# Two levels of Strassen for three quarters of the rope projections, and values weighed by half blocks

## The chip, the cores and the metric

The kernel runs on one core of a Trainium2 chip. A core has a matrix engine (PE, with a queue PEld that loads weights), a vector engine (DVE), a scalar engine (ACT), a general one (POOL), and SP, which here only issues DMAs; each queue runs its instructions in program order, and 16 DMA engines move the data. The metric is device microseconds of one execution, median of the runs shown.

## The reference

The input x is (8, 256, 512), all in float32. It is layer-normed to xn, and two branches follow:

```
q_c, k_c, v_c = up-projections (512 columns each) of 64-wide latents of xn
q_r = xn @ Wq_rope              # 512 x (128 heads * 64): the largest product by far
k_r = xn @ Wk_rope              # 64 columns, shared by the heads
scores = (q_c . k_c + q_r . k_r) / sqrt(68);  attn = softmax(scores)
s = (attn . v_c) @ Wo;   g = silu(ffn(xn));   out = x + s * g
```

The heads are 4 wide (plus 64 for the rope part), there are 128 of them, and a head's scores are 256 x 256.

## The kernel before

**First phase.** `first_phase` norms and transposes x, computes the latents and the gate g, and writes to DRAM what the second phase reads: `xs_d[p]` has, for each pair p of sequences (512 tokens), the seven operands in x of one level of Strassen's algorithm. It also runs the first four units of the projection (`Project`), since the second phase runs ahead by four.

**Second phase.** It walks over 64 blocks n = (sequence b, group sg of 16 heads), two sequences of a pair in turn, and each block in two halves; h = 2n + half numbers the 128 halves. One half does, in this order on PE: `score` twice (96 matmuls with 32 rows of weights and 256 columns each, into 4 banks of PSUM each time), for some blocks `Prepare` (q_c and k_c of a later block), and one unit j = h + 4 of the rope projection (`Chain`). An even half then also weighs the values of the whole previous block (`weigh`, `gather`). A float32 matmul shows as two instructions in the trace, so `score` twice are 96 instructions, a unit is 112, `weigh` of a block 64.

**A unit** is 256 columns of Wq_rope (two sets of 128) by 512 tokens by K = 512. `Chain` makes it of 7 products instead of 8: each has K = 256 (two chunks), 128 output rows in four tiles of 32 array columns (`on_columns`, L173), and 256 moving columns. Their sums gather in four PSUM banks: ACT copies a bank to a fresh one (`seed`) where a partial sum is wanted twice, ACT and DVE carry the four results to `qrs`. The 512 KB of weights come by `load_rope` (L124, two buffers) and the four sums of them by `sum_w`: for the first 32 units POOL computes them (L136 to L139) and SP stores them to `sums_d`; later pairs use the same columns again and load them (L142).

**The softmax** of a half: DVE takes the 8 maxima (L915) as soon as scores are there, ACT the exponentials (L921), DVE transposes them into `rings` (L928), of three slots. `some(k)` places k pairs of exponentials among ACT's copies for the projection; the order of every queue is written by hand (`manual_schedule`).

**Banks.** All PSUM tiles come from one pool of eight banks in rotation: the next one asked for waits until everything that read the bank eight requests earlier is done. An even half asks for 13, an odd one for 12.

**POOL** also builds `qcm` (L307), the masked q_c that `score` of the next block starts with, places values (L348), and adds accumulators (L980). SP's DMAs are in one queue: `load_rope` for unit j + 2 waits there until PE has finished unit j.

Of the kernel before, what the change touches and what calls it, by code (L numbers as in the profile page):

```python
# [9 lines left out]
F32 = mybir.dt.float32  # L10
# [22 lines left out]
EPS = 1e-5  # L33
QSCALE = float((HD + R) ** -0.5)
# [3 lines left out]
def mla_ffn_gate_kernel(  # L38
# [26 lines left out]
    ident = const.tile([P, P], F32, name="ident")  # L65
    make_identity(nc, ident)
# [18 lines left out]
    sums_d = [dram.tile([P, 4, 2, P], F32, name=f"sums_d{n}") for n in range(32)]  # L85
    gates_d = [dram.tile([P, D], F32, name=f"gate_d{n}") for n in range(NT // P)]

    actp = pool("act", 4)
    wp = pool("wrope", 2)
# [3 lines left out]
    wsp = pool("wsum", 2)  # L93
    xsp = pool("xsum", 1)
    qtp = pool("qt", 1)
# [10 lines left out]
    units = 4 * len(blocks) // 2  # L106
    ropes, wsums, xsums = {}, {}, {}
# [10 lines left out]

    def load_rope(j):

        if j < units:
            t = wp.tile([P, KT, 4 * R], F32, tag="w", name=f"w_{j}")
            sg, u = j // 4 % 8, j % 4
            nc.sync.dma_start(out=t, in_=w_rope[sg, u // 2][:, :, ds(u % 2 * 4 * R, 4 * R)])  # L124
            ropes[j] = t

    def sum_w(j):  # L130

        if j < units:
            t = wsp.tile([P, 4, 2, P], F32, tag="ws", name=f"ws_{j}")
            if j < 32:
                q = lambda a, k: ropes[j][:, 2 * k : 2 * k + 2, a::2]
                nc.gpsimd.tensor_add(t[:, 0], q(1, 0), q(1, 1))  # L136
                nc.gpsimd.tensor_sub(t[:, 1], t[:, 0], q(0, 0))
                nc.gpsimd.tensor_sub(t[:, 2], q(0, 0), q(1, 0))
                nc.gpsimd.tensor_sub(t[:, 3], q(0, 1), t[:, 1])  # L139
                nc.sync.dma_start(out=sums_d[j], in_=t)  # L140
            else:
                nc.sync.dma_start(out=t, in_=sums_d[j % 32])  # L142
            wsums[j] = t

    def sum_x(p, xnT):


        q = lambda k, e: xnT[:, 2 * k : 2 * k + 2, ds(e * S, S)]
        for i, of in ((0, q(0, 0)), (1, q(1, 0)), (2, q(1, 1))):
            nc.sync.dma_start(out=xs_d[p][:, i], in_=of)  # L150
        t = {i: xsp.tile([P, 2, S], F32, tag=f"x{i}", name=f"xt{i}_{p}") for i in range(3, 7)}
        for i, one, two in (
            (3, q(0, 1), q(0, 0)),
            (4, q(1, 1), t[3]),
            (5, q(1, 1), q(0, 1)),
            (6, q(1, 0), t[4]),
        ):
            nc.gpsimd.tensor_sub(t[i], one, two)
            nc.sync.dma_start(out=xs_d[p][:, i], in_=t[i])

    def load_xs(p):

        if p < B // 2:
            xsums[p] = {}
            for i in (0, 4, 5, 3, 1, 6, 2):
                xsums[p][i] = xsp.tile([P, 2, S], F32, tag=f"x{i}", name=f"x{i}_{p}")
                nc.sync.dma_start(out=xsums[p][i], in_=xs_d[p][:, i])
# [12 lines left out]
    class Project:  # L180


        def __init__(self, j):
# [3 lines left out]
            self.a = lambda a, k: w[:, 2 * k : 2 * k + 2, a::2]  # L187
            self.x = xsums[j // 32]
# [4 lines left out]
            self.banks = []  # L193
            self.e = [qtp.tile([P, S], F32, tag=f"e{i}", name=f"e{i}_{j}") for i in range(4)]
# [7 lines left out]
        def first(self):  # L202

            for i, (w, x) in enumerate(
                ((self.a(0, 0), 0), (self.s[:, 1], 4), (self.s[:, 2], 5), (self.s[:, 0], 3))
            ):
                self.banks.append(bank(f"q{i}_{self.j}")[:, 0:S])
                product(self.banks[i], w, self.x[x], True)

        def take(self, i):  # L210
            nc.scalar.copy(self.e[i], self.banks[i])

        def join(self):

            m1, m6, m7, m5 = self.e
            nc.gpsimd.tensor_add(m6, m6, m1)
            nc.gpsimd.tensor_add(m7, m7, m6)
            nc.gpsimd.tensor_add(self.out(1, 1), self.split(m7), self.split(m5))

        def second(self):  # L220

            for i, w, x in ((0, self.a(0, 1), 1), (2, self.a(1, 1), 6), (3, self.s[:, 3], 2)):
                product(self.banks[i], w, self.x[x], False)
            nc.scalar.copy(self.out(0, 0), self.split(self.banks[0]))

        def end(self):

            nc.vector.tensor_add(self.out(1, 0), self.split(self.e[1]), self.split(self.banks[2]))
            nc.vector.tensor_add(self.out(0, 1), self.split(self.e[1]), self.split(self.banks[3]))

        def start(self):
            self.first()
            for i in (0, 2, 3, 1):
                self.take(i)
            self.join()

    class Chain(Project):
# [3 lines left out]
        def __init__(self, j):  # L241
            super().__init__(j)
            self.banks = {}

        def product(self, i):

            at, w, x = {
                1: (0, self.a(0, 0), 0),
                5: (3, self.s[:, 0], 3),
                6: (1, self.s[:, 1], 4),  # L250
                2: (0, self.a(0, 1), 1),
                7: (2, self.s[:, 2], 5),
                3: (1, self.s[:, 3], 2),
                4: (2, self.a(1, 1), 6),
            }[i]
            if i in (1, 5):
                self.banks[at] = bank(f"q{at}_{self.j}")[:, 0:S]
            product(self.banks[at], w, self.x[x], i in (1, 5))
# [12 lines left out]
        def add(self, a, e):  # L271
            at = {(1, 1): 2, (0, 1): 1}[a, e]
            nc.vector.tensor_add(self.out(a, e), self.split(self.e[0]), self.split(self.banks[at]))  # L273

# [28 lines left out]
    def spread(n):  # L303

        b, sg = blocks[n]
        qcm = qcp.tile([P, 8, 4, 32], F32, tag="qcm", name=f"qcm_{n}")
        nc.gpsimd.tensor_mul(  # L307
            qcm,
            qks[b, sg // 2][0].rearrange("p (q i) -> p q i", i=32).unsqueeze(2).to_broadcast([P, 8, 4, 32]),
            mask_sb[:, ds(4 * (sg % 2), 4)].unsqueeze(1).unsqueeze(3).to_broadcast([P, 8, 4, 32]),  # L310
        )
        qcms[n] = qcm
# [39 lines left out]
    def first_phase(between):  # L352
        st = ExitStack()
        fw = pool("fw", 1, st)
        wdn_sb = fw.tile([P, KT, P], F32, name="wdn_sb")
# [389 lines left out]
        for tb in range(NTB):  # L745
            more = tb + 1 < NTB
            for u in range(6):
# [9 lines left out]
                if pj:  # L757
                    pj.second()
                    pj.end()
# [20 lines left out]
            else:  # L780
                low_out(tb, 2)
                low_sum(tb)
            gate_out(tb)
# [48 lines left out]
    def between(step):  # L832
# [4 lines left out]
        elif step == 1:  # L837
            load_act(0)
            load_act(1)
            for b in range(2):  # L840
                load_cv(b, qtp.tile([P, S], F32, tag=f"e{b}", name=f"cv_{b}"))
            for j in range(2):
                load_rope(j)
        elif step == 2:
# [4 lines left out]
            spread(0)  # L849
# [4 lines left out]
        elif step < 8:  # L854
            load_rope(step - 2)
            if step < 6:
                sum_w(step - 2)
        else:
            sum_w(4)
            sum_w(5)  # L860
            load_act(2)
# [20 lines left out]
    rings = [tp.tile([P, 3, 8, 4, 32], F32, name=f"ring{r}") for r in range(4)]  # L882
# [3 lines left out]
    def score(n, f):  # L886
# [3 lines left out]
        qcm, qr, kc, a = qcms[n], qrs[n], qks[b, sg // 2][1], acts[b]  # L890
        sc = [bank(f"sc_{n}_{f}_{r}").rearrange("p (h k) -> p h k", h=2) for r in range(4)]

        for part in range(3):
            for h in range(2):
                q = 2 * f + h
                for r in range(4):
                    rows = slice(32 * r, 32 * r + 32)
                    if part == 0:
                        lhs, rhs = qcm[rows, q], kc[rows, :]
# [26 lines left out]
    def transpose(n, f, r):  # L926

        nc.vector.transpose(  # L928
            rings[r][:, (2 * n + f // 2) % 3].rearrange("p k q i -> p q k i")[:, ds(2 * (f % 2), 2)],
# [4 lines left out]
    swapped = {}  # L934

    def weigh(n, halves=range(2)):
# [3 lines left out]
        if 0 in halves:  # L940
            avs[n] = bank(f"av_{n}")
        av = avs[n]
        slots = [(2 * n + half) % 3 for half in halves]
        if len(slots) == 2:
            one, two = sorted(slots)
            of, cols = slice(one, two + 1, two - one), ds(0, S)
            swapped[n] = one != slots[0]
        else:
            of, cols = slice(slots[0], slots[0] + 1), ds(halves[0] * P, P)
            swapped[n] = False  # L950
        for k in range(8):
            for r in range(4):
                nc.tensor.matmul(  # L953
                    av[32 * r : 32 * r + 32, cols],
                    vpad[:, k, r, :],
                    rings[r][:, of, k].rearrange("p h q i -> p h (q i)"),
# [5 lines left out]
    def gather(n, cols=ds(0, S)):  # L962


        b, sg = blocks[n]
        if n not in accs:
            accs[n] = [
                smp.tile([P, S], F32, tag=f"acc{what}{sg % 2}{b % 2}", name=f"acc{what}_{n}", bufs=1)
                for what in range(2)
            ]  # L970
        for what in (1, 0):
            side = (sg + what) % 2
            for to, of in ((early, late), (late, early)) if swapped[n] else ((cols, cols),):
                nc.scalar.activation(  # L974
                    accs[n][what][:, to], avs[n][:, of], AF.Copy, scale=sides_sb[:, side : side + 1]
                )
        if sg % 2:
# [4 lines left out]
    def normalize(n, cols=ds(0, S)):  # L982
# [5 lines left out]
        if n not in recs:  # L988
# [4 lines left out]
        nc.vector.scalar_tensor_tensor(  # L993
            outT[b][:, sg // 2, cols], x[:, cols], 1.0, rec, ALU.mult, ALU.mult
        )
# [46 lines left out]
    for n, (b, sg) in enumerate(blocks):  # L1042
        for half in range(2):
            one, two = 2 * half, 2 * half + 1
            j = 2 * n + half + 4
# [6 lines left out]
            score(n, two)  # L1052
            pre = None
# [11 lines left out]
            pj = Chain(j) if j < units else None  # L1065
            some(5 if pre else 3)
            if pj:
# [3 lines left out]
            some(1)  # L1071
            if pj:
# [4 lines left out]
            if pre:  # L1077
                pre.take()
            else:
                some(1)  # L1080
            if pj:
                pj.give(0, 0)
            some(1)
# [140 lines left out]
```

## Time and profile before

| what | us |
|---|---|
| median of 3 runs (1972.31 to 1972.64) | 1972.62 |
| the profiled execution, its own time | 1973.39 |
| its span, first to last instruction | 1971.5 |
| PE busy in the span | 1959.1 (99%) |
| DVE, ACT, POOL busy | 1576.8, 1120.1, 489.3 |
| first score of half 0 / half 4 / half 25 / half 27 / half 123 | 208.5 / 258.2 / 542.8 / 569.4 / 1900.3 |
| DMA: moved, share of the 16 engines on SP's queue | 186.95 MB, 27.6% |

"Busy" counts an engine's instructions, not its use: PE's instructions overlap, and so their durations (379 ns for one of 256 columns) say less than the distance between their starts. The half starts are those of the first matmul at L902 of each half.

### The profile page before, as it was taken

Reading aid. Unit: us, or ns where it says so; the run is one execution under the profiler, and the core shown is the slowest. Engines: PE = TensorE matmul, PEld = TensorE weight load, DVE = VectorE, ACT = ScalarE, POOL = GpSimd, SP = SyncE. Lnnn points to the kernel's source line nnn. Section 1 sums busy time; section 2 is a strip of 40 time slices with the busy share of each in tenths; the row PEclk is TensorE's granted clock in tenths of the full one; section 3 lists DMA queues with packets and bytes.
Section 4 is the critical chain, followed back from the end, with each engine's and each line's share of the span. In section 5 each row is a group of like instructions: output and inputs, shape, how many; then the busy total and the mean of one; then the engine's idle time right before and its main releaser. Section 6 shows DMA issues by size and latency. Waiting matters only on the chain.

```text
span 1971.5 us, 77380 instructions
## 1 busy us (share of the span) xinstructions
PE 1959.1 (99%) x34007; PEld 1296.3 (66%) x34007; DVE 1576.8 (80%) x2662; ACT 1120.1 (57%) x3031; POOL 489.3 (25%) x741
## 2 busy tenths in 40 slices
PE   9999999999999999999999999999999999999998
PEld 4335677676677666676776766776776767676675
DVE  7764678888887877888887877788787878888888
ACT  4433565655665654656656655556556555655664
POOL 7867343343321112110111111111111111110112
PEclk9999999999999999999999999999999999999999
DMA  6344322222232223222232223222232322122212
GB/s 196 114 136 164 121 98 77 77 83 82 84 118 90 78 92 119 78 88 86 68 125 76 92 87 121 81 88 69 85 118 75 100 88 88 66 88 88 74 49 87
DMA packets 120069, 186.95 MB, mean 95 GB/s; under 512 B 10777, under 2 KB 84905, under 8 KB 119733
## 3 DMA queue, kind: packets, MB, share of 16 engines
q1 hardware_dynamic: 119665, 181.97, 27.6%
q8 instruction: 269, 4.41, 1.0%
q14 instruction: 67, 0.55, 0.1%
q0 software_dynamic: 64, 0.01, 0.0%
q10 hardware_dynamic: 4, 0.01, 0.0%
HBM read 147.86 MB, written 34.10 MB: 92 GB/s over the span
## 4 chain that ended last, share of the span: by engine, by line
PE 95%; DVE 2%; POOL 1%; DMA 1%; issue 1%; ACT 0%; SPq 0%; ACTq 0%; POOLq 0%; DVEq 0%
PE q L173 40%; PE sc L902 34%; PE av L953 11%; PE po L173 2%; PE pf L173 2%; PE py L173 1%; PE px L173 1%; PE pm L173 1%; DVE ring L928 1%; PE qq L287 1%; PE pp L173 1%; DVE nmx L915 1%; PE first L694 0%; PE vps L332 0%; PE pm L647 0%
## 5 line engine op out<-in xcount | busy, mean ns | idle before, releaser
L921 ACT ACTIVATE pr<-sc,nmx 128x256 f32<-128x256 f32 x2048 | 805.4, 495 | 386.2 <-DVE nmx L915 384.5
L915 DVE TENSOR_REDUCE nmx<-sc 128x2 f32<-128x512 f32 x1024 | 635.5, 683 | 253.8 <-PE sc L902 229.1
L928 DVE STREAM_TRANSPOSE ring<-pr 128x512 f32<-128x512 f32 x1024 | 647.6, 680 | 0.0
L173 PE MATMUL q<-x,ws 128*32 128x256 f32 x8192 | 489.1, 379 | 0.7 <-DMA x<-xs_d 0.6
L902 PE MATMUL sc<-act,qr 32*128 32x256 f32 x8192 | 487.6, 374 | 0.0
L902 PEld LDWEIGHTS sc<-act,qr 32*128 32x128 f32 x8192 | 419.8, 185 | 22.2
L173 PE MATMUL q<-x,w 128*32 128x256 f32 x6144 | 404.2, 381 | 1.2 <-ACT vall L340 1.1
L173 PEld LDWEIGHTS q<-x,ws 128*32 128x32 f32 x8192 | 265.2, 110 | 178.1 <-ACT q L262 14.7
L173 PEld LDWEIGHTS q<-x,w 128*32 128x32 f32 x6144 | 179.5, 110 | 164.0 <-ACT pr L921 35.8
L902 PE MATMUL sc<-kc,qcm 32*128 32x256 f32 x4096 | 280.0, 387 | 0.0
L902 PEld LDWEIGHTS sc<-kc,qcm 32*128 32x128 f32 x4096 | 197.4, 184 | 64.9 <-issue 56.5
L953 PE MATMUL av<-ring,vpad 128*32 128x256 f32 (+1 forms) x4160 | 233.4, 376 | 0.1
L953 PEld LDWEIGHTS av<-ring,vpad 128*32 128x32 f32 x4160 | 134.3, 110 | 88.6 <-issue 1.6
L307 POOL TENSOR_TENSOR qcm<-qc,mask_sb 128x1024 f32<-128x1024 f32 x64 | 121.2, 1893 | 253.7 <-PE sc L902 253.7
L980 POOL TENSOR_TENSOR acc<-acc,acc 128x256 f32<-128x256 f32 (+1 forms) x66 | 48.2, 752 | 522.0 <-ACT acc L974 522.0
L974 ACT ACTIVATE acc<-av,sides_sb 128x128 f32<-128x128 f32 (+1 forms) x172 | 60.5, 420 | 192.6 <-PE av L953 192.6
L262 ACT COPY q<-q 128x256 f32<-128x256 f32 x248 | 88.5, 357 | 121.5 <-PE q L173 121.5
L273 DVE TENSOR_TENSOR qr<-e,q 128x256 f32<-128x256 f32 x248 | 99.5, 401 | 52.1 <-PE q L173 52.1
L348 POOL COPY vpad<-vall 32x128 f32<-32x128 f32 x256 | 75.9, 296 | 260.9 <-PE av L953 240.7
L269 ACT COPY qr<-q 128x256 f32<-128x256 f32 x248 | 100.5, 405 | 4.8 <-PE q L173 4.7
L136 POOL TENSOR_TENSOR ws<-w 128x256 f32<-128x256 f32 x32 | 27.0, 844 | 180.3 <-DMA w<-in_w_rope_dram 118.9
L1027 POOL TENSOR_TENSOR g<-g,xr 128x512 f32<-128x512 f32 x15 | 19.0, 1270 | 211.1 <-DVE g L1026 186.0
(138 smaller groups left out, 1032.6 us busy)
## 6 DMA issues: line engine op xcount, KB each, us to landing
w<-in_w_rope_dram SPq DMA_DIRECT2D x128, 512.0 KB
ws<-sums_d SPq DMA_DIRECT2D x96, 512.0 KB
sums_d<-ws SPq DMA_DIRECT2D x32, 512.0 KB
x<-xs_d SPq DMA_DIRECT2D x28, 256.0 KB
xt<-in_x_dram SPq DMA_DIRECT2D x16, 256.0 KB
xs_d<-xt SPq DMA_DIRECT2D x16, 256.0 KB
gate_d<-gs SPq DMA_DIRECT2D x16, 256.0 KB
g<-gate_d SPq DMA_DIRECT2D x16, 256.0 KB
```

The costliest lines, as they stand in the source:

```text
L173: nc.tensor.matmul(to[tile_], w[:, tile_], x, start=start, stop=stop, skip_group_check=True)
L262: nc.scalar.copy(self.banks[i], self.banks[i - 1])
L269: nc.scalar.copy(self.out(a, e), self.split(self.banks[at]))
L273: nc.vector.tensor_add(self.out(a, e), self.split(self.e[0]), self.split(self.banks[at]))
L307: nc.gpsimd.tensor_mul(qcm, qks[b, sg // 2][0].rearrange("p (q i) -> p q i", i=32).unsqueeze(2).to_broadcast([P, 8, 4, 32]), mask_sb[:, ds ...
L348: nc.gpsimd.tensor_copy(vpad[rows, :, :, 8 * t + 4 * (sg % 2) :][..., :4], valls[b][rows, :, sg])
L902: nc.tensor.matmul(sc[r][:, h, :], lhs.rearrange("p t i -> p (t i)"), rhs, start=(part == 0 and h == 0), stop=(part == 2), skip_group_chec ...
L915: nc.vector.tensor_reduce(nmx[:, r, :], scs[n, f][r], AX.X, ALU.max, negate=True)
L921: nc.scalar.activation(p[:, h, :], scs[n, f][r][:, h, :], AF.Exp, bias=nmxs[n, f][:, r, h : h + 1])
L928: nc.vector.transpose(rings[r][:, (2 * n + f // 2) % 3].rearrange("p k q i -> p q k i")[:, ds(2 * (f % 2), 2)], prs.pop((n, f, r)).rearran ...
L953: nc.tensor.matmul(av[32 * r : 32 * r + 32, cols], vpad[:, k, r, :], rings[r][:, of, k].rearrange("p h q i -> p h (q i)"), start=(k == 0), ...
L974: nc.scalar.activation(accs[n][what][:, to], avs[n][:, of], AF.Copy, scale=sides_sb[:, side : side + 1])
```

## The change

Pair 0 (units 0 to 31) keeps the one-level `Chain`, one half further ahead (j = h + 5; the first phase runs a fifth unit). For the pairs 1, 2 and 3 two units and two levels make one double unit of 49 inner products instead of 2 * 7 * 2 = 28 chunk products: `Twice(m, part)`; one part is done in a half, part 0 with three of the seven outer products at a time and part 1 with four. An inner product has K = 128 and 128 moving columns (168 and 224 instructions for part 0 and 1). Inner sums gather in four banks as in `Chain`; ACT, POOL (`join`) and DVE (`end`) carry the quadrants to SBUF, and POOL joins the outer products there (`outer`: one addition of 128 x 512 after part 0, six after part 1).

The second level's operands are made once, by POOL, and kept in DRAM. They are made one at a time beside the halves 0 to 22 ("asides"): for units 28 to 31 the first-level sums, ahead of their halves (`EarlySums`), for pairs 1 to 3 the sums in x (`InnerX`), for the 16 double units the sums in the weights (`InnerW`). Each loads its operands into one buffer `staged` (16 KB a partition), computes in place, and stores.

Values are weighed by half blocks, one half later (`weigh(n, half)`: 64 instructions of 128 columns, in every half), so `rings` has two slots instead of three, and `spread` makes half of `qcm` at a time. In `normalize` the last product moves from DVE to POOL. Many tiles now share one SBUF tile `mix`.

```diff
+    def raw_sums(q, to):
+        nc.gpsimd.tensor_add(to[0], q(1, 0), q(1, 1))
+        nc.gpsimd.tensor_sub(to[1], q(0, 0), q(1, 0))
+        nc.gpsimd.tensor_sub(to[2], to[0], q(0, 0))
+        nc.gpsimd.tensor_sub(to[3], q(0, 1), to[2])
...
+    def load_w2(n):
+        m, part, k = ONCE // 2 + n // 14, n // 7 % 2, n % 7
+        if m < 64:
+            i, of = ORDER[k], slice(512 * part, 512 * part + 512)
+            to = slots(n % NRING)
...
+                nc.sync.dma_start(out=to, in_=w2_d[m % 16][:, W_SUM[i], of])
...
+    class Twice:
...
+        def product(self, i):
+            k = ORDER.index(i)
+            n = 14 * (self.m - ONCE // 2) + 7 * self.part + k
+            if i in (1, 5):
+                self.open(AT[i])
+            to, x, w = self.banks[AT[i]], x2_tile(self.part, k), w2.pop(n)
+            for o in range(self.count):
...
+                on_columns(to[:, o], of, x[:, o], i in (1, 5) and o == 0, True)
+            load_w2(n + NRING)
...
+        def seed(self, i):
+            self.open(i)
+            nc.scalar.copy(self.banks[i], self.banks[i - 1])
...
+        def join(self):
+            nc.gpsimd.tensor_add(self.mine[:, :, 3], self.w, self.five)
+        def end(self):
+            nc.vector.tensor_add(self.mine[:, :, 1], self.five, self.banks[1])
+        def outer(self):
...
+            if self.part == 0:
+                give_q(0, 0, one, two)
+            else:
+                add(six, one)
+                add(seven, six)
+                give_q(1, 0, seven, four)
+                give_q(1, 1, seven, five)
+                add(five, six)
+                give_q(0, 1, five, three)
...
-        nc.vector.scalar_tensor_tensor(
-            outT[b][:, sg // 2, cols], x[:, cols], 1.0, rec, ALU.mult, ALU.mult
-        )
+        nc.gpsimd.tensor_mul(outT[b][:, sg // 2, cols], x[:, cols], rec)
...
+    staged = more["x2"][:, 0 : 32 * P].rearrange("p (c m) -> p c m", c=4)
...
+    class InnerW:
+        def load(self):
+            for u in range(2):
+                j = 2 * self.m + u
+                for k in range(2):
+                    to = staged[:, 2 * u + k]
+                    nc.sync.dma_start(
+                        out=to[:, 0:512].rearrange("p (k m) -> p k m", k=2), in_=rope(j)[:, k::2]
+                    )
+                    nc.sync.dma_start(
+                        out=to[:, 512:1024].rearrange("p (o m) -> p o m", o=4), in_=sums_d[j][:, :, k]
+                    )
+        def make(self):
+            q = lambda u, k: staged[:, 2 * u + k]
+            raw_sums(q, [q(1, 1), q(1, 0), q(0, 0), q(0, 1)])
+        def store(self):
+            nc.sync.dma_start(out=w2_d[self.m], in_=staged)
...
+    asides = [EarlySums(j) for j in range(28, 32)]
+    asides += [InnerX(1)] + [InnerW(m) for m in (0, 1, 2, 3, 14, 4, 15, 5, 6)]
+    asides += [InnerX(2), InnerW(7), InnerW(8), InnerX(3)] + [InnerW(m) for m in range(9, 14)]
...
+            if h < 2 * last + 1:
+                spread(*((n, 1) if half == 0 else (n + 1, 0)))
...
+            once = h + 5 < ONCE
+            some((5 if pre else 3) if once else (6 if pre else 4))
...
+            else:
+                tw = Twice(ONCE // 2 + (h - ONCE + 5) // 2, (h - ONCE + 5) % 2)
+                tw.product(1)
+                tw.product(5)
+                weigh(*back, range(4))
+                tw.seed(1)
+                tw.product(6)
+                some(1)
+                tw.product(2)
+                weigh(*back, range(4, 6))
+                tw.seed(2)
+                if pre:
+                    pre.take()
+                else:
+                    some(1)
+                tw.product(7)
+                tw.take(7)
+                tw.product(3)
+                weigh(*back, range(6, 8))
+                some(2)
+                tw.take(1)
+                tw.take(5)
+                tw.join()
+                tw.product(4)
+                for f in (one, two):
+                    for r in range(4):
+                        transpose(n, f, r)
+                tw.end()
+                tw.take(4)
+            if h:
+                gather(*back, back[0] < last)
+            if half == 0 and n >= 1:
+                place_values(n)
+            if not once and h < 123:
+                tw.outer()
...
+            if once:
...
+                sum_w(j + 1)
+                load_rope(j + 2)
+            if h - 1 in asides:
+                asides[h - 1].make()
+                asides[h - 1].store()
+            if h in asides:
+                asides[h].load()
```

## The prediction

> **What bounds the kernel now.** I read the busy table first, then the timeline of one block late in the run, then the few matmuls of 128 columns, then SP's queue and POOL in pair 0, where the change puts new work. The page, with four of its groups and one of the answer by form:
>
> ```profile
> PE 1959.1 (99%) x34007; PEld 1296.3 (66%) x34007; DVE 1576.8 (80%) x2662; ACT 1120.1 (57%) x3031; POOL 489.3 (25%) x741
> q1 hardware_dynamic: 119665, 181.97, 27.6%
> L307 POOL TENSOR_TENSOR qcm<-qc,mask_sb 128x1024 f32<-128x1024 f32 x64 | 121.2, 1893 | 253.7 <-PE sc L902 253.7
> L348 POOL COPY vpad<-vall 32x128 f32<-32x128 f32 x256 | 75.9, 296 | 260.9 <-PE av L953 240.7
> ```
>
> PE is the bound; the DMA engines work a quarter of the time, at 181.97 MB / (0.276 * 1971.5 us) = 334 GB/s while they work. The timeline (start, duration, engine, line; PE alone):
>
> ```profile
> 1000.27 1.15 PE L902 MATMUL sc<-kc,qcm 32*128 32x256 f32 x16
> 1005.66 1.07 PE L173 MATMUL q<-x,w 128*32 128x256 f32 x16
> 1011.73 3.64 PE L953 MATMUL av<-ring,vpad 128*32 128x256 f32 x64
> 1015.30 1.15 PE L902 MATMUL sc<-kc,qcm 32*128 32x256 f32 x16
> 1026.87 1.15 PE L902 MATMUL sc<-kc,qcm 32*128 32x256 f32 x16
> ```
>
> An even half takes 15.03 us (scores 5.39, projection 6.07, weighing 3.57), an odd one 11.57: 26.60 a block, all of it PE. Four column tiles run together, and sets of four start 0.216 us apart at 256 columns ((3.64 - 0.38) / 15). At 128 columns, at the end of the run:
>
> ```profile
> 1948.74 1.95 PE L953 MATMUL av<-ring,vpad 128*32 128x128 f32 x64
> ```
>
> Here the starts, read one by one, are 0.133 once and then 0.109 apart. Last, one unit's load in pair 0, on SP and on POOL:
>
> ```profile
> 271.00 0.55 SPq L124 DMA_DIRECT2D w<-in_w_rope_dram  x1
> ```
>
> ```profile
> 275.07 0.84 POOL L136 TENSOR_TENSOR ws<-w 128x256 f32<-128x256 f32 x1 [6.34 <-DMA w<-in_w_rope_dram]
> 275.99 0.74 POOL L137 TENSOR_TENSOR ws<-ws,w 128x256 f32<-128x256 f32 x1
> ```
>
> 512 KB (524 kB) need 4.07 us from issue to use; at 334 GB/s 1.57 of that is moving, so 2.5 us is fixed.
>
> **Asides, halves 0 to 22: the part that decides.** `InnerW` loads 8 * 256 KB = 2.1 MB into `staged`, POOL makes four sums of 1024 columns in place, SP stores 2.1 MB from there. There is one `staged`, so the next load waits until the store has landed: load, sums and store follow each other and never overlap.
> - Load: 2.5 + 2.1 MB / 334 GB/s = 8.8. Store: the same, 8.8.
> - Sums: POOL's contiguous additions take 0.77 us at 256 columns (L980) and 1.28 at 512 (L623, L635 to L637), so 1.28 + 512 * 0.0021 = 2.35 at 1024; four are 9.4. The row of 1024 columns (L307, one input a broadcast mask) would give 1.89, 7.6 in all; I take the first, since its inputs are alike.
> - One aside is thus T = 27.0 us; `InnerX` (896 columns, 1.84 MB) 8.0 + 8.4 + 8.0 = 24.4. `EarlySums` is 4.1 + 2.9 + 5.7 and fits a half.
>
> The halves take 13.58 us here (284.6 us from half 4 to half 25). The asides are in the same queues as work that PE needs. On SP, the store waits for POOL's sums and the next aside's load for the landed store; `load_rope` of the following half stands behind them. On POOL the sums wait for the load, and behind them stands `spread`, without which the next scores can't start: the aside loaded in half h holds the `spread` for half h + 3. So half h + 3 starts no earlier than load(h) + 8.8 + 9.4 + 1.0 (half of L307). The first load, in half 4, can start some 19 us into that half (rope load there at 12.8, then a 512 KB store with the rope load before it). The last, in half 22, comes 15 * 27.0 + 3 * 24.4 = 478 later, and half 25 starts 19 + 478 + 19 = 516 us after half 4 instead of 284.6: **+232 us**. Two halves of lead (some 24 us) are used up in this already. Ends: POOL by the 1024 row and moving at 375 GB/s (the best slice early in the run), T = 23.8 and +173; POOL a tenth slower and 280 GB/s, T = 30.6 and +297.
>
> The Trainium skill (DMA: Bandwidth & Descriptors, Anatomy of one DMA) gives about 2.0 us fixed and bytes / 436 GB/s for a DMA on another path; by it a load and a store are 6.8 each, T = 23 and the term an estimated +160. No run here shows that rate over 2 MB.
>
> Bytes alone speak the same way: 4.2 MB for the aside and 1.05 MB of pair 0's own are 15.7 us at 334 GB/s, more than a half. That weighing is spread evenly over pair 0's halves hides under this pace.
>
> **The double units, halves 27 to 122 (48 blocks' worth).** PE: 56 sets at 0.216 become 98 at 0.109: 12.10 to 10.68 us. Weighing is 16 * 0.216 or 32 * 0.109, no difference. -1.42 a block, **-68 us** if PE stays the bound.
>
> The Trainium skill says (TensorE: Matmul & The Clock Gate, Part 3, The mechanism) that a weight load overlaps matmuls in flight only where the row group differs. The four tiles here share it. By that rule a set would cost its load (0.110, PEld's row) on top of its stream, some 0.22, and the double units 9 us more a block, an estimated +440. The run of 64 above disagrees: 0.109 a set, with a load for each instruction.
>
> ACT gets six copies of 384 or 512 columns a half instead of five of 256, and its order now matters. In the timeline the first exponentials come 3.61 us into a half, a pair takes 0.72, a copy is free again after 0.27 (256) to 0.49 (512) and its result is there after 0.36 to 0.59; ACT reads a bank 0.3 after PE's last start. In part 0: exponentials to 6.49, seed, pair (7.6), second seed after product 6 (8.53), pair (9.63), take(7) after product 7 (10.26), two pairs (12.08), take(1) done at 12.56. The next half's fourth score bank is the one that take(1) frees (13 requests a half, 8 banks), so that half starts at 12.3, where PE would be done at 5.39 + 4.54 + 1.73 = 11.66. Part 1: 13.6 against 13.17. In halves with `Prepare`, output or `values` PE has enough besides. Half of the 0.43 and 10/16 of the 0.64: 0.61 a block, **+29 us**.
>
> POOL does part 1's six outer additions (1.28 each) after takes that end 14.4 us into the even half, after `join` (1.28), `place_values` (1.24) and, by block, accumulators (1.54) or the normalizing product (0.75). Only then comes `spread` for the block after. It is done at 28.3, 26.5, 26.0 or 27.3 us by n mod 4, where the next block would start at 26.5, 25.95, 26.5, 25.95. Mean 0.93, for the 10/16 of blocks without other work: 0.58, **+28 us**. With POOL's slower rows (L158, 1.37 to 1.50) it is +60.
>
> Sum here: -68 + 29 + 28 = **-11**; ends -68 (neither wait shows) and +21.
>
> **The rest.** Seven loads of 256 KB a half are 5.5 us of moving in some 12.8; each is asked for a whole half ahead and needs 3.3: hidden, by 9 us; if that cover goes, a product waits. The fifth unit in the first phase adds 112 instructions (6.1 us) and half 123 loses as many: 0. DVE loses a product of 0.56 every second block, and a block's four additions of 256 become one of 384 and one of 512: it is at 80% and behind no wait of PE.
>
> **Sum.** 1973.4 (the profiled execution, 0.8 over the median) + 232 - 11 = 2194, as a median some 2193.
>
> **Rivals.**
> - The asides hide, and the kernel is faster. For it: in halves 4 to 24 the DMA engines are busy 24% and POOL 99 of 284.6 us; SP waits mostly for PE (1210.7 us at L124). Half 25 comes about 18 T + 37 us after half 4, so it needs T under 14.4 us (18 T + 37 - 284.6 < 11), or under 17.5 with the whole -68. Against: the sums alone are 7.6 to 9.4. Time 1962, down to 1905.
> - Load and store overlap the sums in some way that I overlooked, and DMA bytes set T = 15.7: +35, time 1997. Against: one buffer, written and read whole.
> - PE itself loses: sets at 0.133 (the first distance of the run of 64) instead of 0.109, through strided weights or waits between short products. 98 * 0.133 + 32 * 0.133 against 12.10 + 3.46: +1.73 a block, +83, with ACT's and POOL's waits covered; time 2288. It turns the double units into a loss above 0.12 a set.
>
> **How the numbers follow.** As described 0.80, its own range 2077 (173, -68) to 2290 (297, +21); overlapped 0.08; hidden 0.05; PE loses 0.07. The range takes the first and last of these, and a little of what lies below the first: 2035 to 2300. 0.2% (4 us) is what a measurement here can tell from no change: faster 0.05, same 0.01, slower 0.94.
>
> **What would show it.** Right: from half 4 to 25 about 516 us, halves of 24 to 28 us from about half 8 on, PE busy about half there with its granted clock below full, its waits ended by POOL (`qcm`) or by the rope weights' DMA, SP waiting for POOL's sums. Later, blocks of 25.5 to 27 us, sets of 128 columns at 0.109, the first scores of a half waiting for ACT's copies and some for `qcm`. Wrong: halves 4 to 22 still near 13.6, or aside stores that land while the next load already runs. A rate over 334 GB/s or quicker sums would shrink the first term 18 us for each us of T.

## The result, and the profile after

The changed kernel takes 2263.11 us (median of four runs, 2258.34 to 2266.8) against 1972.63: a ratio of 1.1471 [1.1449, 1.1493], 290 us more. The prediction was 2193 us, in a range of 2035 to 2300. The profiled execution took 2258.34 us, 284.95 more than the profiled one of before; the rest of this section is about these two.

First the busy table, two rows of the slices, SP's DMA queue and three groups from the page of the changed kernel:

```profile
PE 1991.3 (88%) x46103; PEld 1632.7 (72%) x46103; DVE 1559.7 (69%) x2533; ACT 1263.1 (56%) x3211; POOL 1219.1 (54%) x1339
PE   9998995565755499999999999999999999999988
PEclk9999997777887699999999999999999999999999
q1 hardware_dynamic: 302001, 343.95, 46.8%
L1137 PE MATMUL sc<-kc,qcm 32*128 32x256 f32 x4096 | 351.1, 408 | 210.0 <-POOL qcm L467 207.7
L467 POOL TENSOR_TENSOR qcm<-qc,mask_sb 128x512 f32<-128x512 f32 x128 | 133.2, 1041 | 4.9 <-PE sc L1137 4.9
L508 POOL COPY vpad<-vall 32x128 f32<-32x128 f32 x256 | 73.7, 288 | 33.8 <-PE av L1179 23.1
```

PE was busy 99% of the span before and is busy 88% now. POOL's work grew from 489 to 1219 us, the bytes on SP's queue from 182 to 344 MB, and PE stood 207.7 us in front of the score matmuls for `qcm`, which POOL builds. The row of slices says where: in slices 7 to 14 (of 40, 338 to 790 us) PE is half empty, and there too the granted clock is below full.

The two traces laid against each other by the starts of the first score matmul of a half:

| stretch | before | after | difference | predicted |
|---|---|---|---|---|
| up to half 0 (first phase) | 208.5 | 227.8 | +19.3 | 0 (6.1, given back by half 123) |
| half 0 to 4 | 49.7 | 51.5 | +1.8 | 0 |
| half 4 to 25 (asides) | 284.6 | 516.9 | **+232.3** | +232 |
| half 25 to 27 | 26.6 | 28.6 | +2.0 | 0 |
| half 27 to 123 (double units) | 1330.9 | 1356.1 | **+25.2** | -11 |
| half 123 to the end | 71.2 | 75.6 | +4.4 | 0 |
| sum | 1971.5 | 2256.5 | +285.0 | +221 |

The largest term is as predicted; the rest is 64 us worse than predicted. Busy times by stretch (from:to, length, then busy time and instructions of PE, PEld, DVE, ACT, POOL, then granted clock, DMA share and GB/s):

```profile
279.30:796.20 516.90, 321.99 (x5816) 237.07 (x5812) 229.90 (x393) 175.39 (x491) 273.24 (x231) 0.80 0.56 195
824.80:2180.90 1356.10, 1313.62 (x35268) 1205.62 (x35264) 1068.08 (x1713) 919.77 (x2338) 738.01 (x795) 1.00 0.47 145
```

In the stretch of the asides no engine is full: PE is busy 62%, POOL 53%, the DMA engines 56%. That is what a chain of work looks like that goes from one engine to the next and back.

**One aside.** The timeline of the changed kernel from one stored aside to the next (start, duration, engine, line), SP's and POOL's rows and the first score matmuls:

```profile
603.66 0.33 SPq L1090 DMA_DIRECT2D w_d<-x  x1
...
612.04 0.55 SPq L1078 DMA_DIRECT2D x<-in_w_rope_dram  x1
...
616.62 0.61 SPq L1081 DMA_DIRECT2D x<-sums_d  x1
...
617.99 0.95 SPq L159 DMA_DIRECT2D mix<-in_w_rope_dram  x1
...
622.94 2.34 POOL L164 TENSOR_TENSOR x<-x 128x1024 f32<-128x1024 f32 x1 [15.43 <-DMA sums_d<-mix]
...
630.20 2.34 POOL L167 TENSOR_TENSOR x<-x 128x1024 f32<-128x1024 f32 x1
...
632.49 1.04 POOL L467 TENSOR_TENSOR qcm<-qc,mask_sb 128x512 f32<-128x512 f32 x1
632.56 0.33 SPq L1090 DMA_DIRECT2D w_d<-x  x1
...
633.59 2.09 PE L1137 MATMUL sc<-kc,qcm 32*128 32x256 f32 x16 [12.96 <-POOL qcm L467]
...
640.95 3.38 SPq L1102 DMA_DIRECT2D x<-xs_d  x4
```

The store is issued at 603.66, and the next load, which writes where the store reads, at 612.04. The sums start at 622.94, 10.9 us after the load's first issue, and take 9.6. Directly behind them on POOL stands `qcm` (632.49), and the score matmul starts the moment it is there, after 12.96 us of waiting. At 632.56 the sums are stored, and the next aside's load follows at 640.95, 8.4 us later. Load, sums and store never overlap. What PE and SP waited for in this stretch, from 340 us on (engine, line, releaser: us in total, times, longest):

```profile
PE sc L1137 <- POOL qcm L467: 170.8, 16, 13.0
```

```profile
SPq L1090 <- POOL x L167: 145.4, 15, 9.8
SPq L1078 <- DMA w_d<-x: 86.6, 13, 8.1
```

SP spends 145.4 us with a store that waits for POOL and 86.6 with a load that waits for the store to land, and the rope weights of the next units wait behind both.

**The double units.** A part of the timeline late in the run:

```profile
1501.52 1.93 PE L205 MATMUL r<-x,mix 128*32 128x128 f32 x64
...
1519.18 1.04 POOL L467 TENSOR_TENSOR qcm<-qc,mask_sb 128x512 f32<-128x512 f32 x1
...
1520.28 1.33 PE L1137 MATMUL sc<-kc,qcm 32*128 32x256 f32 x15 [0.87 <-POOL qcm L467]
```

In the first row 64 instructions are 16 sets of four; their starts, read one by one, are 0.109 us apart (1501.520, .630, .739 and so on), through strided operands and with a weight load for each. The last row has PE waiting for the half of `qcm` that POOL builds only after its outer additions. Over the whole stretch this wait shows as

```profile
PE sc L1137 <- POOL qcm L467: 31.2, 23, 2.3
```

The 96 halves from 27 to 122, each cut by the starts of its matmuls into the first `score`, the second, the gap to the projection, projection with weighing, and the gap to the next half's first score (sums in us; `early_spread` and `takes_early` are experiments told below):

| part of the halves 27 to 122 | before | after | early_spread | takes_early |
|---|---|---|---|---|
| first score | 239.8 | 264.2 | 270.4 | 246.2 |
| second score | 248.6 | 258.7 | 260.9 | 250.3 |
| gap to the projection | 29.2 | 29.2 | 29.2 | 29.2 |
| projection, `Prepare`, output, weighing | 782.1 | 747.3 | 747.2 | 756.3 |
| gap to the next score | 31.2 | 56.8 | 22.6 | 22.6 |
| sum | 1330.9 | 1356.1 | 1330.3 | 1304.6 |

The scores are the same instructions on the same data in all four, so what they take over 239.8 and 248.6 is waiting. Of the 24.4 us by which the first score grew, 18.6 arise within its first four instructions, which are the first to write its four banks; that these are waits for banks is tested below, by takes_early.

### The profile page after: what moved, and what is told of

Same layout as the page of the kernel before. It is cut to its first block, busy times and chain, and to the rows that moved or that the text cites. A ratio compares the mean times of both kernels' runs of the same rounds, so it can differ in the third digit from the quotient of the medians.

```text
span 2256.5 us, 103982 instructions
## 1 busy us (share of the span) xinstructions
PE 1991.3 (88%) x46103; PEld 1632.7 (72%) x46103; DVE 1559.7 (69%) x2533; ACT 1263.1 (56%) x3211; POOL 1219.1 (54%) x1339
## 4 chain that ended last, share of the span: by engine, by line
PE 52%; POOL 24%; DMA 11%; ACT 4%; SPq 4%; DVE 3%; issue 2%; POOLq 0%; ACTq 0%; DVEq 0%
PE sc L1137 19%; PE r L205 15%; PE av L1179 5%; POOL mix L424 5%; POOL qr L422 5%; DMA w_d<-x 5%; PE q L205 4%; PE po L205 2%; ACT mix L404 2%; DMA sums_d<-mix 2%; ACT pr L1156 2%; SPq L1078 2%; POOL x L167 2%; POOL x L165 2%; POOL x L166 2%
## 5 line engine op out<-in xcount | busy, mean ns | idle before, releaser
L205 PE MATMUL r<-x,mix 128*32 128x128 f32 x17280 | 542.0, 273 | 5.3 <-issue 5.1
L1137 PE MATMUL sc<-kc,qcm 32*128 32x256 f32 x4096 | 351.1, 408 | 210.0 <-POOL qcm L467 207.7
L205 PEld LDWEIGHTS r<-x,mix 128*32 128x32 f32 x17280 | 472.2, 110 | 43.8 <-issue 27.3
L407 POOL TENSOR_TENSOR mix<-mix 128x384 f32<-128x384 f32 x96 | 109.3, 1138 | 581.9 <-ACT mix L404 581.9
L1179 PE MATMUL av<-ring,vpad 128*32 128x128 f32 x8192 | 287.6, 273 | 2.8 <-issue 2.0
L422 POOL TENSOR_TENSOR qr<-mix 128x512 f32<-128x512 f32 x192 | 244.1, 1282 | 11.3
L205 PE MATMUL q<-mix 128*32 128x256 f32 x3584 | 210.3, 389 | 36.3 <-DMA mix<-sums_d 24.9
L404 ACT COPY mix<-r 128x512 f32<-128x512 f32 (+1 forms) x384 | 188.6, 564 | 67.9 <-PE r L205 67.3
L205 PEld LDWEIGHTS q<-mix 128*32 128x32 f32 x3584 | 115.0, 112 | 128.9 <-issue 42.3
L424 POOL TENSOR_TENSOR mix<-mix 128x512 f32<-128x512 f32 x144 | 184.1, 1279 | 11.4
L467 POOL TENSOR_TENSOR qcm<-qc,mask_sb 128x512 f32<-128x512 f32 x128 | 133.2, 1041 | 4.9 <-PE sc L1137 4.9
```

Of the source, the lines that this page charges most:

```text
L205: nc.tensor.matmul(to[tile_], w[:, tile_], x, start=start, stop=stop, skip_group_check=True)
L404: nc.scalar.copy(to, self.banks[at])
L407: nc.gpsimd.tensor_add(self.mine[:, :, 3], self.w, self.five)
L422: nc.gpsimd.tensor_add(to, v(x), v(y))
L424: add = lambda x, y: nc.gpsimd.tensor_add(x, x, y)
L467: nc.gpsimd.tensor_mul(qcm, qks[b, sg // 2][0].rearrange("p (f q i) -> p f q i", f=2, i=32)[:, half].unsqueeze(2).to_broadcast([P, 4, 4, 32]),
```

## Experiments on the asides

The theory: an aside costs load plus sums plus store, since there is one buffer, and holds both queues while it runs. The rivals: DMA bytes alone set the pace; POOL's sums alone set it; or it is only the place of `spread` behind the sums on POOL.

**no_asides.** All asides go; the double units read other operands of the same size.

```diff
-            if j < 28:
+            if j < 32:
...
-    asides = {k: of for k, of in enumerate(asides)}
+    asides = {}
```

> Leaves the asides out: the second-level sums are not made, and the double units load first-level operands of the same sizes from DRAM in their place (so the projection of the last three pairs has wrong operands and the right amount of work); pair 0's halves make all 32 first-level sums. Theory (load, sums and store in series on one buffer, with SP and POOL held behind them): halves 4 to 25 go from 517 us back to 285 +- 5, everything else stays, 2263 - 232 = 2031 us. Rival (part of the loss in pair 0 comes from weighing by halves, the shared tile or the half spreads): more than 300 us stay between half 4 and half 25, over 2050 in all.

Measured: 2026.35 us, ratio 1.0274 [1.0244, 1.0304]. From half 4 to half 25:

```profile
278.10:562.00 283.90, 283.69 (x5817) 213.76 (x5812) 229.52 (x391) 174.50 (x489) 98.75 (x155) 1.00 0.24 80
```

The 233 us are gone, to less than a microsecond of the stretch before the change, and PE is full again at full clock. The halves 27 to 122 took 1363.7 us here, 7.6 more than in the changed kernel, with operands read from other places; I did not follow that up, and go by the stretch.

**dma_only** and **sums_only.** Each keeps one side of an aside. The first loads and stores without POOL's sums, the second makes the sums without loads and stores (and the double units read what they do in no_asides); the four small asides of pair 0 stay whole in both.

```diff
             if h - 1 in asides:
-                asides[h - 1].make()
+                if isinstance(asides[h - 1], EarlySums):
+                    asides[h - 1].make()
```

> The asides for pairs 1 to 3 load and store but leave their four POOL sums out (the stored operands are the raw ones). Theory of a serial chain: T falls from 28.9 to load 10.9 + store 8.4 = 19.3 us and stays above the 13.6 of a half; half 4 to 25 about 370 us (19 + 15 * 19.3 + 3 * 17.5 + 7), 2115 us in all. Rival (POOL alone is the bound, its sums 9.6 beside 5.2 of its own work): back to 285, 2031. Rival (the DMA engines' moving alone is the bound): still about 517, 2263.

```diff
                 asides[h - 1].make()
-                asides[h - 1].store()
+                if isinstance(asides[h - 1], EarlySums):
+                    asides[h - 1].store()
-            if h in asides:
+            if h in asides and isinstance(asides[h], EarlySums):
                 asides[h].load()
```

> The asides for pairs 1 to 3 keep POOL's four sums (on a buffer filled with zeros) and leave their loads and stores out; the double units load first-level operands of the same sizes instead. Theory of a serial chain: POOL has 9.6 + 5.2 = 14.8 us of work a half against 13.4, of which the lead hides most: half 4 to 25 290 to 305 us, 2036 to 2051 in all. Rival (POOL and its queue are the bound): near 517 us, 2263.

Measured: dma_only 2119.16 us, 1.0745 [1.0713, 1.0776]; sums_only 2060.84 us, 1.0449 [1.0419, 1.0479]. dma_only from half 4 to 25, then its waits of PE and of SP:

```profile
279.00:653.80 374.80, 306.57 (x5814) 225.90 (x5810) 230.59 (x394) 175.93 (x489) 99.33 (x155) 0.91 0.79 276
```

```profile
PE q L205 <- DMA mix<-in_w_rope_dram: 41.4, 10, 7.9
```

```profile
SPq L1078 <- DMA w_d<-x: 100.2, 13, 10.4
```

sums_only from half 8 to 22 and its one wait of PE there:

```profile
340.50:559.70 219.20, 200.45 (x3876) 150.66 (x3876) 155.37 (x264) 115.62 (x324) 199.40 (x166) 0.95 0.21 70
```

```profile
PE sc L1141 <- POOL qcm L470: 22.2, 6, 4.3
```

Half 4 to 25 takes 374.8 us with the DMAs alone (+90.9 over no_asides) and 318.3 with the sums alone (+34.4). Both together, in series, cost 233, which is 108 more than the two of them added. Neither rival can give the 232 us by itself. Loading and storing alone come to about 19 us per aside ((374.8 - 37) / 18, by the prediction's count), more than a half. sums_only took 13 us more than the upper end expected: I had POOL fit beside PE, but in these halves it is busy 199.4 of 219.2 us, 14.2 a half, more than the 13.5 that a half takes in no_asides, and with the waits for `qcm` behind the sums a half comes to 15.7.

**early_spread.** `qcm` for the next block is made a half earlier, ahead of the aside's sums on POOL.

```diff
-            if h < 2 * last + 1:
-                spread(*((n, 1) if half == 0 else (n + 1, 0)))
+            if n < last:
+                spread(n + 1, half)
```

> The whole change, with the masked q_c of a half made one half earlier (two halves ahead instead of one), so that it no longer stands behind POOL's outer additions. Theory: in halves 27 to 122 the 36 us in which the first scores wait for it go (25 to 36 in all, since ACT's copies may hold the same banks a little later); the asides hold the rope weights and their first-level sums just as much, so half 4 to 25 stays within 500 to 517; 2220 to 2238 in all. Rival (the asides hurt by holding this one operand): half 4 to 25 falls by over 50 us. Rival (the doubles lose nothing through POOL's order): under 10 us of change in halves 27 to 122.

Measured: 2222.38 us, 1.1268 [1.1235, 1.1301]. From half 4 to 25 it still takes 509.7 us. PE's waits there:

```profile
PE q L205 <- POOL mix L164: 110.3, 15, 10.2
PE q L205 <- DMA mix<-in_w_rope_dram: 36.0, 11, 5.2
PE q L205 <- DMA mix<-sums_d: 35.2, 2, 22.4
```

The wait for `qcm` is gone, and waits for the first-level sums of pair 0 (also on POOL, behind the aside's) and for rope weights (on SP, behind the aside's store) stand in its place. The name in the waits of the changed kernel was therefore not the cause: the queues are held by the asides, and whatever stands next in them is what PE waits for. Moving one of these saves 7 us of 232.

## Experiments on the double units

**early_spread again.** In the halves 27 to 122 that kernel took 1330.3 us instead of 1356.1: 25.8 us less. The gap ahead of the scores fell by 34.2 us, and 8.4 of that came back in the score matmuls, presumably as waits for banks instead.

**takes_early.** early_spread, and ACT copies two banks to SBUF as soon as they are whole, ahead of work that the next half's scores do not need.

```diff
+                tw.take(5)
                 tw.seed(2)
...
                 tw.product(7)
+                tw.take(1)
                 tw.take(7)
...
                 some(2)
-                tw.take(1)
-                tw.take(5)
                 tw.join()
```

> The whole change with the half-early masked q_c, and with two of ACT's six copies of a double unit moved into gaps of ACT's queue: the copy of product 5 ahead of the second seed, that of products 1 and 2 ahead of take(7), where both stood behind the last exponentials. Theory (the first scores of the next half wait for banks that these two copies free, 31 + 12 us of the halves 27 to 122 with the half-early q_c): 15 to 32 us of these go, halves 27 to 122 fall from 1330 to 1298 to 1315, about 2197 in all. Rival (the banks are late for the last exponentials themselves, so the copies' place does not matter): under 8 us.

Measured: 2192.79 us, 1.1116 [1.1094, 1.1138]; the halves 27 to 122 take 1304.6, 25.7 less again (last column of the table). The scores fell by 34.8 us together, and 9.1 came back within the projection. With both orders mended the double units gain 26.3 us on the kernel before. So the arithmetic pays, and in the changed kernel two orders of queues gave it away.

**one_level.** All four pairs by `Chain`, no asides, no double units: what is left is the unit more in the first phase, the weighing by half blocks, the product moved to POOL.

```diff
-ONCE = 32 * 1
+ONCE = 32 * 4
...
-    asides = {k: of for k, of in enumerate(asides)}
+    asides = {}
```

> No second level at all: all units by the one-level chain and no asides; weighing by halves, the half spreads, the shared tile, the product moved to POOL and the fifth unit in the first phase stay. Theory: the first phase keeps its +18 (half 0 near 227), the weighing costs nothing, the end loses nothing: 1991 us (1985 to 1997). Rival (weighing by halves, with twice the instructions, costs PE a few per cent): blocks over 27.0 us, over 2010 in all.

Measured: 1998.23 us, 1.013 [1.011, 1.015], 1 us over the range. Half 0 starts at 226.2 (208.5 before), halves 4 to 25 take 283.8 (284.6), and halves 27 to 122 take 1339.4 (1330.9). Weighing by half blocks is free in ordinary blocks (13.32 + 13.32 us against 15.03 + 11.57). What costs is the first phase, +17.7, and the halves with the output's projection with the half after them: 16.8 plus 13.9 to 14.5 against 15.0 plus 15.0.

This run is also the closer measure of the double units, since it weighs by half blocks as they do: against its 1339.4 us they lose 16.7 in the changed kernel and gain 34.8 with both orders mended.

In the first phase, PE waits for (waits of the changed kernel up to 228 us):

```profile
PE q L205 <- POOL mix L164: 6.3, 1, 6.3
PE q L205 <- ACT mix L253: 2.7, 5, 0.6
```

The fifth unit, at the end of the phase, waits 6.3 us for first-level sums that POOL makes only then; with its 6.1 us of matmuls and small waits it takes 15, and the new order of copies in `Project` costs some 2.4 to 3.6 more (the first phase of two_pairs below, 213.0 us, less those of two_pairs_b and two_pairs_c, which have the order of before).

## Looking for a faster version

If the double units gain 26 us over three pairs and the asides and the first phase cost 252, a version with fewer asides, further apart, might win. Three were run.

**two_pairs.** Double units for the last two pairs alone, asides in every third half, both orders mended, and the extra unit as a `Chain` in half 0.

```diff
-ONCE = 32 * 1
+ONCE = 32 * 2
...
-    asides = {k: of for k, of in enumerate(asides)}
+    asides = {3 * k + 2: of for k, of in enumerate(asides)}
```

> A version by what the runs show: the one-level chain for pairs 0 and 1, the double units for pairs 2 and 3; an aside every third half (18 over halves 2 to 53) in place of every half; the half-early q_c and the two copies moved; the fifth unit in half 0 instead of the first phase. Theory: an aside of 28.9 us in 40 us of halves holds nothing, so the halves before the doubles go at 13.4 to 13.7; the doubles (64 halves) gain some 0.3 a half, 19 in all; the first phase keeps about 4: 1960 us (1950 to 1975), faster than before. Rival (DMA traffic or POOL's sums cost PE even where no queue is held): the halves before the doubles at 14 or more, 1990 or over.

Measured: 1993.49 us, 1.0109 [1.0093, 1.0126], a miss. The double halves (59 to 122) behaved as expected: 862.3 us against 885.0. But half 0 to 4 took 61.9 instead of 49.7: 6.1 for the unit, and of the rest the trace gives 2.4 to a wait for rope weights. And the halves 27 to 58 took 473.4 instead of 445.9: PE waits 10.5 us for first-level sums of the rope weights, whose loads stand on SP behind an aside's store, and SP waits 88.4 us there for POOL. The halves from 4 to 58 take 14.3 us each, which the rival had as its sign; two_pairs_b, which in the halves 27 to 58 moves the store alone, takes 16 of these us back, so the held queue is a good part of it.

**two_pairs_b.** The store half a block later, the first four units in the order of before, and the extra unit in half 1 from weights loaded ahead.

```diff
             if h - 1 in asides:
                 asides[h - 1].make()
-                asides[h - 1].store()
+            if h - 2 in asides:
+                asides[h - 2].store()
```

> two_pairs with three places mended that its trace shows: an aside is stored one half later, when its sums are long done, so that SP no longer stands in wait for POOL in front of the rope weights (some 24 us in halves 27 to 58); the fifth unit runs in half 1 on the asides' buffer, loaded when the second phase begins, so that it delays no other unit's weights (4 us); the four units of the first phase go by the order they had before (3.5 us). Theory: 1993 - 32 = 1961 us (1954 to 1970), 0.6% faster than before. Rival (pair 1's late weights come from the DMA engines being busy, not from SP's wait): halves 27 to 58 keep their 15 to 19 us, over 1980.

Measured: 1988.89 us, 1.0092 [1.0076, 1.0109], a miss again. The halves 27 to 58 fell from 473.4 to 457.4 us and the first phase to 210.6, but the extra unit's weights were late (half 1 took 32.0 us: their DMA stands on SP behind 32 small loads and is issued 10 us into that half) and half 27 took 19.7.

**two_pairs_c.** The lead of four halves is kept up to half 28, and that half runs two units.

```diff
-            j = h + 5
+            j = h + 4 + (h >= 28)
...
+            if h == 28:
+                pj = Chain(32)
...
```

> two_pairs_b with the projection one unit less ahead (four, as before the change) until half 28, which runs two units, the second on the asides' buffer; no aside is in flight near half 27, where pair 1's operands in x are loaded. Theory: the first phase and halves 0 to 4 cost nothing more than before (11 to 21 us less than in two_pairs_b), half 28 costs 6 more, the doubles keep their -22 and the end its -2: 1972 - 22 - 2 + 6 + 4 = 1958 us (1951 to 1968), 0.7% faster than before. Rival (the one-level halves with an aside beside every third cost 10 us and more through the DMA engines): 1970 or over.

Measured: 1981.09 us, 1.0049 [1.0035, 1.0062]: nearer, and still slower. The double halves gain 16.1 us (868.9 against 885.0), the end 2.2. Half 0 to 28 loses 14.4 (386.9 against 372.5), 8.4 of it in half 26, where POOL's first-level sums are late (PE's waits, half 0 to 59):

```profile
PE q L205 <- POOL mix L164: 6.0, 1, 6.0
```

Half 28 to 59 loses 10.4, 8 of it for the two units of half 28, and the first phase 0.9. The time is the rival's (1970 or over), but its cause is not: half 4 to 25, with an aside in every third half or oftener, takes 287.1 us, 3 more than no_asides. So no version that beats the kernel before was found. Whether one exists with the last of these stalls mended stays open; by the terms above I estimate about a tie.

## Why the prediction came out as it did

**The asides: right, in its mechanism and its size.** The stretch grew by 232.3 us where +232 stood; the first load came 19.1 us into half 4 (19 predicted; one of its four DMAs went ahead, at 14.3), and the last 476.9 us after it (478). The three experiments show the two parts of the mechanism separately: the order in series (34 + 91 becomes 233) and the held queues (early_spread). The split of T was off, with errors that cancelled, and so the agreement to a microsecond is luck. For the weights a load takes 9.9 to 11.9 us to the first sum, 10.8 in the mean, instead of 8.8; sums 9.6 instead of 9.4; store to next load 6.2 to 8.4, 7.0 in the mean, instead of 8.8. The three means add up to the 27.5 us that pass from one aside in the weights to the next (27.0 predicted), with no matmul among them; the asides in x took 21.4 to 21.9 instead of 24.4. That the store was cheaper than the load is what the prediction's equal prices missed. Part of it shows in the timeline: SP needs 5.2 us to issue a load's eight DMAs (612.04 to 617.23), and 0.33 for the store's one. The estimate from the Trainium skill (DMA: Bandwidth & Descriptors, Anatomy of one DMA), 6.8 us for either, is near the store's mean here (7.0) and 4 short for the load. Two small slips of the working change little: 284.6 us over 21 halves are 13.55 each and not 13.58, and the slow end's T comes to 30.3 and not 30.6 (+292).

**The double units: the PE term right, the waits under-sized, and one left out.** The term was -68 for PE, +29 for banks, +28 for POOL's order; measured +25.2 instead of -11, outside the ends -68 to +21.
- PE: the fastest plain halves give 15.20 to 14.06 us a block for projection and weighing (-55 over 48 blocks), and the two gaps ahead of the scores 0.61 to 0.40 (-10): -65 against -68. The rival in which PE loses did not happen: 97 of 100 sets start 0.109 to 0.110 after the one before. The rule of the Trainium skill that the prediction weighed (TensorE: Matmul & The Clock Gate, Part 3, The mechanism), by which weight loads in one row group would show, is not borne out for these tiles.
- Banks: the scores grew by 34.5 (24.4 and 10.1), predicted 29. takes_early took 34.8 out of them.
- POOL's order: the gap ahead of the scores grew by 25.6 where PE alone would have made it 10 smaller, so some 36, predicted 28. early_spread took 34.2 out.
- Left out: projection and weighing fell by 34.8, not by 55: some 20 us of waits between the products, 0.2 a half. The prediction let ACT hold the next half's banks, but not the products' own. takes_early, which moved copies, made this part 9.1 us longer, which points at ACT's order; which copy holds which product was not separated.

**The rest: "0" failed.** The step said that the fifth unit's 6.1 us come back in half 123. The unit takes 15 us, as it waits for sums that nothing prepares ahead, and `Project` lost 2.4 to 3.6 besides; one_level shows the 17.7 without any double unit or aside. At the other end nothing came back in the changed kernel: half 123 to the end grew by 4.4. In one_level it is 2.6 shorter than before, and in early_spread 1.8 (69.4 us), so some 6 us of this are POOL's order again. The cover named for the loads of 256 KB (a whole half of lead) held: no group of PE's waits in halves 27 to 122 names them.

**The rivals.** That the asides hide falls with T at 27.5. That bytes set T at 15.7 falls twice: DMAs alone need 19, and bytes were not the limit (DMA share 0.56).

Of the 64 us by which the sum was short, 36 are the halves of the double units and 19 the first phase; the remaining 8 lie about the asides' ends and at the run's end.

## What to carry to other kernels

Work that is made ready "beside" a loop must fit into one iteration on every queue that it passes, and with a single buffer load, compute and store have to be added, not compared: 34 and 91 us became 233. Where an engine's wait names a small operation, look at what stands ahead of that operation in its queue; moving the small one only changes the name. When matmuls get shorter, the copies that free their banks and the operands of the next iteration become late first: here their order in two queues was worth 52 us, twice what the arithmetic gained once it was mended.

## What the runs showed of the hardware that I had not expected

In these four runs the mean granted clock falls with PE's busy share. In the stretch of the asides:

| kernel, stretch | PE busy | granted clock |
|---|---|---|
| no_asides, half 4 to 25 | 100% | 1.00 |
| sums_only, half 8 to 22 | 91% | 0.95 |
| dma_only, half 4 to 25 | 82% | 0.91 |
| changed kernel, half 4 to 25 | 62% | 0.80 |

These are means of two values, full and half: in the changed kernel the trace has the clock at half for 40% of this stretch and at full for the rest. Two windows of it, the first from within the wait for `qcm` that ends at 604.68:

```profile
599.70:609.90 10.20, 5.21 (x48) 4.39 (x52) 0.00 (x0) 0.00 (x0) 7.66 (x7) 0.50 0.49 206
609.95:623.50 13.55, 10.68 (x228) 7.34 (x220) 12.71 (x21) 8.15 (x23) 0.56 (x1) 1.00 0.73 232
```

The 48 instructions of the first score take 5.3 us to the second score's start, at half the clock, and those of the second 2.7 to the projection's, at full. The prediction had only said "below full". It did not set the time of this stretch, whose 27.5 us an aside add up without a matmul; ACT's and DVE's busy times there (175.4 and 229.9 us) are those of no_asides (174.5 and 229.5).

And the two transfers of an aside, of 2.1 MB each, differed: the store out of one tile, in rows of 16 KB by one DMA, had landed and the next load was issued in 6.2 to 8.4 us, while the load into the same tile, in eight DMAs of 512-byte and 1 KB pieces, took 9.9 to 11.9 to the first use. Which of direction, piece size and number of DMAs makes the difference was not separated.
